# Mixing one batch directly ahead of another batch's scores, with other product steps and another beginning, in a fused decoder layer

## The chip, the cores and the metric

The kernel runs on one core of one Trainium2 chip. The metric is the device time of one execution in microseconds (us); the time before is the median of three runs.

## The reference

A decoder layer (self-attention, cross-attention to a context, MLP) is followed by a gated cross-attention to the same context. There are 16 batches of 128 tokens, 512 features, 16 heads of 32, all in float32.

```python
ln_out = layernorm(hidden_states, ln1_s, ln1_b)
q, k, v = jnp.split(ln_out @ w_qkv + b_qkv, 3, axis=-1)
ctx = merge_heads(attention(split_heads(q), split_heads(k), split_heads(v), ltor_mask))
x = hidden_states + ctx @ w_ao + b_ao
q = layernorm(x, ln2_s, ln2_b) @ w_q + b_q
k, v = jnp.split(encoder_states @ w_kv + b_kv, 2, axis=-1)
x = x + merge_heads(attention(split_heads(q), split_heads(k), split_heads(v), cross_mask)) @ w_co + b_co
x = x + gelu(layernorm(x, ln3_s, ln3_b) @ w1 + b1) @ w2 + b2
...
a = _layer_norm(audio_kv, ln_gamma, ln_beta)          # the same context
out = softmax_attention(hidden_states @ Wq.T, a @ Wk.T, a @ Wv.T, mask)
return hidden_states + jnp.tanh(gate) * (out @ Wo.T)
```

## The kernel before

**Stages and names.** The 16 batches form four groups of four (512 tokens). Self-attention is called A, the decoder's cross-attention B, the MLP C, the gated cross-attention D. A *section* is one group in one attention. `attend` is called twice: the decoder run has eight sections (A groups 0 to 3, then B groups 0 to 3, 32 batches), and after the MLP the gates' run has the four sections of D (16 batches).

**Order.** Every engine gets its instructions in the order in which the program writes them (`InOrder`), so the order below is the order in each engine's queue. Nothing is scheduled by a planner.

**Steps.** `attend` counts steps k; a section is 16 steps, a batch four, and one step is one *unit* of four heads. Batch b's units 4b to 4b+3 go through a pipeline: scores for all 16 heads at step 4b (`scores`, tile sc, 32 matmuls with 32 rows), scaling and masking of one unit per step, least value and exponential one step later, division by the sum two steps later, and three steps later `turn_unit`, which transposes 32x32 squares on VectorE and sends the unit to DRAM (tile away). `receive_pair` brings two units back with four DMAs on SyncE's queue, so that probabilities arrive transposed (tile pT, three buffers). It runs at step pair + 5, that is 4b+6 and 4b+8. `mix` multiplies them with the values (tile av, 32 matmuls of 32 columns) at step 4b+10, in the middle of a batch's four steps; its copy out of PSUM (`mixed_out`, ScalarE, tile mT) is put off to the next step by `afterwards` and `due`. The out-projection (mo) follows at the next step that starts a batch, 4b+12. In the gates' run the last batch isn't sent: TensorE turns it (`turn_by_array`) and it is mixed seven steps after its first unit's step.

**Products.** Beside the softmax of one section TensorE makes the queries, keys and values of the next. Each 512x512x512 product is split into seven quarter products (one level of Strassen's scheme), numbered 1 to 7, of eight 128x256 matmuls each. `block_product` puts 1, 6 and 7 into PSUM bank mm0 with a copy by ScalarE, 5 and 3 into mm1, 2 and 4 into the two pt buffers, with additions on VectorE one step later. Tables (`BLOCKS`, `SECOND_BLOCKS`, `CROSS_BLOCKS`, `GATED_BLOCKS`, `DEFERRED_BLOCKS`, and `FIRST_BLOCKS` for the first section) say at which step which quarter product is issued; `blocks_plan` turns them into lists. Sums of weights and of activations that the scheme needs run on GpSimd (tiles sums) or VectorE. In D the out-projections of groups 0 to 2 are deferred: their mixed tiles go to DRAM and come back, `added_product` makes them beside group 3 (mm_o_D), and `add_later` makes their sums on GpSimd.

**Beginning.** `SelfAttention.begin` loads x, normalizes group 0 batch by batch (statistics on VectorE, the power on GpSimd), transposes each batch on TensorE (tp_A), and copies the four transposed tiles out whole (`transposed_out`, ScalarE and VectorE in turn, tile T_A). `start` then issues seven query and seven key quarter products (mm_q_A, mm_k_A) before the first scores.

Of the kernel before, what the change touches and what calls it, by code (L numbers as in the profile page):

```python
# [10 lines left out]
F32 = mybir.dt.float32  # L11
# [5 lines left out]
P = 128  # L17
# [7 lines left out]
KC = H // P  # L25
GB = 4
# [27 lines left out]
def decoder_then_gated_cross_attention(ctx: ExitStack, tc: tile.TileContext, a: dict, out: bass.AP):  # L54
# [24 lines left out]
    def afterwards(engine, do):  # L79
        late[engine].append(do)  # L80
# [31 lines left out]

    for b in range(GB):
        load_batch(0, b)
# [37 lines left out]
    def col(name, c):  # L152
        cols, row = columns[name]
        return cols[:, row + c : row + c + 1]
# [3 lines left out]
    w["sq"] = load_weight(a["L0_xattn_w_qkv"], 0, 0, "w_sq")  # L158
# [49 lines left out]
    def normalize(src, dst, name, then):  # L208

        mv = work.tile([P, 2], F32, tag="mv", name=f"mv_{name}", bufs=4)  # L210
        st = work.tile([P, 6], F32, tag="st", name=f"st_{name}", bufs=4)
        nc.vector.bn_stats(st, src)
        nc.vector.bn_aggr(mv, st)
        rstd = work.tile([P, 1], F32, tag="rstd", name=f"rstd_{name}", bufs=4)
        nc.vector.tensor_scalar(rstd, mv[:, 1:2], EPS, None, ALU.add)
        nc.gpsimd.tensor_tensor(rstd, rstd, mhalf[:, 0:1], ALU.pow)

        def rest():
            to, of = (by_chunk(dst), squares(src)) if len(dst.shape) == 4 else (dst, src)
            nc.vector.tensor_scalar(to, of, mv[:, 0:1], rstd, ALU.subtract, ALU.mult)  # L220
            then()

        def rest_by_act():

            off = work.tile([P, 1], F32, tag="off", name=f"off_{name}", bufs=4)
            nc.vector.tensor_scalar(off, mv[:, 0:1], rstd, -1.0, ALU.mult, ALU.mult)
            nc.scalar.activation(by_chunk(dst), squares(src), AF.Identity, bias=off, scale=rstd)
            afterwards("dve", then)

        afterwards("dve", rest if at_start[0] else rest_by_act)  # L230
# [16 lines left out]
    def normalize_and_send(src, dst, away, name, b, then=None):  # L247
        def turn_and_send():
            nc.vector.transpose(dst, dst)
            send(away, dst, b)  # L250
            if then is not None:
                then()

        normalize(src, dst, f"{name}_{b}", turn_and_send)
# [50 lines left out]

    def transposed_out(t, tp, scale, bias):
        for k in range(KC):
            if k % 2 == 0:
                nc.scalar.activation(t[:, k, :], tp[k], AF.Identity, bias=col(bias, k), scale=col(scale, k))
            else:  # L310
                nc.vector.tensor_scalar(t[:, k, :], tp[k], col(scale, k), col(bias, k), ALU.mult, ALU.add)
# [149 lines left out]
    def by_quarters(t):  # L461
# [4 lines left out]
        {1: (1, 2), 2: (6,), 3: (7, 5), 5: (4,), 6: (3,)},  # L466
        {5: (1,), 6: (2,), 7: (6,), 9: (7, 5), 10: (4,), 13: (3,)},
        {10: (1,), 11: (6, 2), 13: (7,), 14: (5,), 15: (4, 3)},
    )

    FIRST_BLOCKS = (
        {0: (1, 2), 1: (6, 5), 2: (7, 4), 3: (3,)},
        {3: (1,), 4: (6, 2), 5: (7, 5), 6: (4, 3)},
    )
    SECOND_BLOCKS = (
        {4: (1, 2), 5: (6, 5), 6: (7, 4), 8: (3,)},
        {7: (1, 2), 8: (6,), 9: (7, 5), 10: (4,), 11: (3,)},
        {12: (1,), 13: (6, 2), 14: (7, 5), 15: (4, 3)},
# [3 lines left out]
        {6: (1,), 7: (6, 2), 9: (7, 5), 10: (4,), 11: (3,)},  # L482
        {11: (1,), 13: (6, 2), 14: (7, 5), 15: (4, 3)},
    )
    GATED_BLOCKS = (
        {0: (1,), 1: (2, 6), 2: (5, 7), 3: (4,), 5: (3,)},
        {5: (1,), 6: (2, 6), 7: (7,), 8: (5,), 9: (4,), 10: (3,)},
        {11: (1, 2), 12: (6,), 13: (5, 7), 14: (4,), 15: (3,)},
# [4 lines left out]
        {12: (1,), 13: (2, 6), 14: (5, 7), 15: (4,), 17: (3,)},  # L493
    )

    def blocks_plan(products, blocks, as_listed=False):
        out = {}
        for jobs, steps_ in zip(products, blocks):
            for step, ns in steps_.items():
                out.setdefault(step, []).extend((not as_listed and n not in (1, 6, 7), jobs[n]) for n in ns)  # L500
        return [([job for _, job in sorted(jobs, key=lambda j: j[0])], [step] * len(jobs)) for step, jobs in out.items()]
# [107 lines left out]
    def mix(bt):  # L609
        sec, b = bt.sec, bt.b  # L610
        av = ps("mm", f"av_{bt.name}")
        for c in range(KC):
            for j in range(GB):
                h = c * GB + j
                nc.tensor.matmul(
                    av[j * HD : (j + 1) * HD, c * S : (c + 1) * S], sec.v[:, b, h * HD : (h + 1) * HD],
                    bt.pT[j][:, :, c, :], start=True, stop=True,
                )
        mT = work.tile([P, KC, S], F32, tag="s", name=f"mT_{bt.name}", bufs=7) if bt.by_array else sec.mixed_tile(b)

        def mixed_out():
            if sec.v_bias is None:
                nc.scalar.copy(mT, av.rearrange("p (c q) -> p c q", q=S))
            else:
                for c in range(KC):
                    nc.scalar.activation(
                        mT[:, c], av[:, c * S : (c + 1) * S], AF.Identity, bias=col(sec.v_bias[0], sec.v_bias[1] + c)
                    )

        afterwards("act", mixed_out)  # L630
        bt.mT = mT
# [30 lines left out]
    def attend(sections, ready, others, after=None):  # L662
# [9 lines left out]

        def by_transfer(n):

            return min(n, (len(sections) * GB - 1) * GB) if ready else n

        def step(k, bt=None, jobs=(), ahead=None):

            m = k % GB
            pair = k - 5  # L680
            if pair % 2 and 0 <= pair < by_transfer(len(units)):
                receive_pair(*units[pair])
            if m == 0 and bt is not None:
                scores(bt)
            due()
            for job in jobs:
                job()
            last_mix = ready and k == by_transfer(k) + 7
            if last_mix:
                mix(batches[-1])  # L690
                projected.append(batches[-1])
            if projected and (m == 0 or ready and bt is None):
                before = projected.popleft()
                if before.by_array:
                    out_project_last(before)
                elif before.sec.deferred:
                    afterwards("act", lambda: before.sec.put_away(before))
                else:
                    out_project(before)
            done = k // GB - 2  # L700
            first_turned = ready and k == by_transfer(k) + 6
            if first_turned:
                turn_by_array(*units[k - 3])
            if m == 2 and 0 <= done < len(batches) - ready:
                mix(batches[done])
                projected.append(batches[done])
# [22 lines left out]
        for i, sec in enumerate(sections):  # L729
            last = i + 1 == len(sections)  # L730
            jobs = others() if last else sections[i + 1].jobs()
# [25 lines left out]
    class SelfAttention(Section):  # L757
# [19 lines left out]
        def begin(self, following):  # L777
# [3 lines left out]
            tp = []  # L781
            for b in range(GB + 1):
                if b == 1:
                    turn_vectors(0)
                    tp += [ps("sc", f"tp_A0_{k}") for k in range(KC)]
                left = late["dve"].popleft() if b else None
                if b < GB:
                    normalize(x[0][:, b, :], ln[:, b, :], f"A0_{b}", lambda b=b: transpose_batch(tp, ln, b))
                if left is not None:
                    left()  # L790
# [11 lines left out]
            for o in SelfAttention.weight_sums[0]:  # L802
                nc.gpsimd.tensor_tensor(*o)
            following.prepare(0)
            at_start[0] = False
            transposed_out(self.lnT, tp, "ln1_s", "ln1_b")

        def start(self, following):

            self.begin(following)  # L810
            _, todo = self.tiles()
            for o in todo:
                nc.vector.tensor_tensor(*o)
            key_sums, value_sums = self.weight_sums[1:]
            prepare = [lambda p=p: following.prepare(p) for p in (2, 4, 6, 9)], [0, 1, 2, 5]
            jobs = plan(
                *blocks_plan(self.products(), FIRST_BLOCKS), prepare,
# [28 lines left out]
        def jobs(self):  # L846
# [3 lines left out]
            if g > 1:  # L850
# [4 lines left out]
                *blocks_plan(first.products()[2:], FIRST_BLOCKS), (sums, [2, 3, 4, 5]),  # L855
# [33 lines left out]
    class CrossAttention(Section):  # L889
# [34 lines left out]
        def jobs(self):  # L924
# [9 lines left out]
            if g == 0:  # L934
# [6 lines left out]
                ([lambda c=c: self.query_chunk(c) for c in range(KC)], [1, 2, 3, 5]),  # L941
                *blocks_plan(products, CROSS_BLOCKS), ([lambda: mask_terms(self.ms, self.ma)], [7]),
# [18 lines left out]
        def weights_begin(self):  # L961
# [13 lines left out]
            def v_sum(n):  # L975
# [6 lines left out]
                ([lambda n=n: v_sum(n) for n in range(4)], [9, 10, 11, 12]),  # L982
# [406 lines left out]
    class GatedAttention(Section):  # L1389
# [110 lines left out]
        def jobs(self):  # L1500
# [16 lines left out]
            elif g == 3:  # L1517
                more = self.deferred_start()
            return plan(
                *blocks_plan(products, GATED_BLOCKS, True), ([by_pool(o) for o in a_sums], [0, 1, 2, 3]), ([mask], [9]), *more  # L1520
# [32 lines left out]
        def deferred_jobs(self):  # L1553
# [6 lines left out]
            def product(g, n):  # L1560
# [11 lines left out]
                ([lambda g=g: add_later(g) for g in (1, 2) for _ in range(4)], [0, 1, 2, 3, 8, 9, 9, 10]),  # L1572
                *blocks_plan(later, DEFERRED_BLOCKS, True),
# [134 lines left out]
```

## Time and profile before

| | |
|---|---|
| median of three runs | 1166.83 us (1165.11 to 1167.07) |
| profiled execution, its own time | 1168.78 us |
| its span, first to last instruction | 1167.0 us |
| mean granted TensorE clock | 0.994 |
| PE (TensorE matmul) busy | 1134.5 us, 97% |
| DVE (VectorE) busy | 739.2 us, 63% |
| ACT (ScalarE) busy | 605.6 us, 52% |
| POOL (GpSimd) busy | 701.5 us, 60% |
| DMA | 259.80 MB, mean 223 GB/s |
| first scores start | 39.73 us |

SP is SyncE, whose queue issues nearly all DMAs; SPq and PEq are the queues' own rows. A row of the timeline gives the start, the duration, the engine, the operation with output <- inputs, the shapes, the number of instructions in the row, and in brackets the idle time before it with what ended it. All operations pass through one helper, so every row has line L50, and tiles tell them apart. Suffixes A, B, C and D name the stage. The profiled execution is one run: its durations are held against its own time, 1168.78.

### The profile page before, as it was taken

What the parts mean: (1) busy time and instruction counts of PE and PEld (TensorE: products, weight loads), DVE (VectorE), ACT (ScalarE), POOL (GpSimd) and SP (SyncE); (2) the same over time, 40 slices, a digit from 0 to 9 for tenths busy, and PEclk for the clock granted to TensorE, in tenths of its full rate; (3) what the DMA queues carried; (4) which work ended last, traced back from release to release, by engine and by line L of the source; (5) the groups of instructions that cost most, each with busy time, mean ns of one, the idle gap of its engine ahead of it and who ended that gap; (6) DMA issues with size and microseconds to landing.
All of it is one profiled execution on the core that took longest, in us unless ns stands there. A gap on an engine that the chain in (4) does not pass through costs nothing. (4 is left out here: it accounts for less than half of the span.)

```text
span 1167.0 us, 22047 instructions
## 1 busy us (share of the span) xinstructions
PE 1134.5 (97%) x7210; PEld 868.3 (74%) x7210; DVE 739.2 (63%) x1894; ACT 605.6 (52%) x2132; POOL 701.5 (60%) x636
## 2 busy tenths in 40 slices
PE   7999999999999999998999999999999999999988
PEld 5877777657575757545788888888888777878866
DVE  7678878797878877876663633543432247767753
ACT  2467667666666766674221333232222247867653
POOL 7698878688868776684333424433341367545973
PEclk9999999999999999999999999999999999999989
DMA  6598979999889879898796696696457728988964
GB/s 227 148 221 220 240 188 222 248 235 267 199 229 208 239 202 255 243 290 252 264 287 235 188 273 197 193 301 224 154 184 249 211 48 229 249 215 251 264 191 163
DMA packets 325266, 259.80 MB, mean 223 GB/s; under 512 B 83544, under 2 KB 280608, under 8 KB 320288
## 3 DMA queue, kind: packets, MB, share of 16 engines
q1 hardware_dynamic: 325112, 258.38, 78.0%
q8 instruction: 58, 0.95, 0.3%
q14 instruction: 56, 0.46, 0.1%
q10 hardware_dynamic: 40, 0.01, 0.0%
HBM read 163.94 MB, written 94.37 MB: 221 GB/s over the span
## 5 line engine op out<-in xcount | busy, mean ns | idle before, releaser
L50 ACT ACTIVATE s_A<-s_A,mn_A 128x128 f32<-128x128 f32 x256 | 99.5, 393 | 51.5 <-issue 37.3
L50 DVE TENSOR_TENSOR h<-h,h 128x512 f32<-128x512 f32 x80 | 54.9, 686 | 112.6 <-PE h L50 112.6
L50 ACT ACTIVATE s_B<-s_B,mn_B 128x128 f32<-128x128 f32 x256 | 99.5, 393 | 46.6 <-issue 32.5
L50 ACT ACTIVATE h<-h 128x512 f32<-128x512 f32 x64 | 40.3, 630 | 160.6 <-DVE h L50 160.6
L50 POOL TENSOR_TENSOR s_D<-s_D,sum_D 128x512 f32<-128x512 f32 x64 | 66.5, 1040 | 67.8 <-DVE sum_D L50 66.3
L50 ACT ACTIVATE s_D<-s_D,mn_D 128x128 f32<-128x128 f32 x256 | 99.2, 392 | 0.4 <-issue 0.4
L50 POOL TENSOR_TENSOR s_B<-s_B,sum_B 128x512 f32<-128x512 f32 x64 | 66.8, 1045 | 48.7 <-DVE sum_B L50 44.3
L50 POOL TENSOR_TENSOR s_A<-s_A,sum_A 128x512 f32<-128x512 f32 x64 | 66.6, 1041 | 36.0 <-DVE sum_A L50 35.3
L50 POOL TENSOR_TENSOR s_A<-s_A,ma 128x512 f32<-128x512 f32 x64 | 81.9, 1280 | 5.4 <-DVE s_A L50 3.7
L50 POOL TENSOR_TENSOR s_B<-s_B,mask 128x512 f32<-128x512 f32 x64 | 81.3, 1270 | 2.1 <-DMA away_B<-s_B 0.4
L50 POOL TENSOR_TENSOR rstd_aD<-rstd_aD,mhalf 128x1 f32<-128x1 f32 x12 | 6.6, 548 | 114.6 <-DVE rstd_aD L50 101.1
L50 POOL TENSOR_TENSOR sh<-h 128x512 f32<-128x512 f32 x32 | 40.7, 1272 | 50.9 <-ACT h L50 43.0
L50 PE MATMUL mo_B<-w_co,mT_B 128*128 128x512 f32 x128 | 60.5, 616 | 2.1 <-ACT mT_B L50 2.1
L50 PE MATMUL h<-T_C,t 128*128 128x256 f32 x256 | 60.7, 380 | 1.4 <-DVE h L50 1.4
L50 PE MATMUL h<-T_C,w 128*128 128x256 f32 x256 | 61.0, 381 | 0.8 <-DVE h L50 0.8
L50 PE MATMUL h<-sx,t 128*128 128x256 f32 x256 | 60.6, 380 | 0.0
L50 PE MATMUL o<-w,h 128*128 128x256 f32 x256 | 60.5, 379 | 0.0
L50 PE MATMUL o<-t,h 128*128 128x256 f32 x256 | 60.5, 379 | 0.0
L50 PE MATMUL o<-t,sh 128*128 128x256 f32 x256 | 60.5, 379 | 0.0
L50 PE MATMUL mo_A<-w_ao,mT_A 128*128 128x512 f32 x128 | 59.1, 604 | 0.0
L50 DVE CUSTOM_DVE_ANT_0 s_D<-sc_D,gmask 128x128 f32<-128x128 f32 x256 | 57.2, 283 | 0.9 <-DMA turned_x<-x_D 0.9
L50 PE MATMUL mm_q_B<-T_B,w_cq 128*128 128x512 f32 x128 | 57.3, 595 | 0.0
(324 smaller groups left out, 2986.1 us busy)
## 6 DMA issues: line engine op xcount, KB each, us to landing
t<-kept SPq DMA_DIRECT2D x24, 1024.0 KB, 6.9
away_A<-s_A SPq DMA_DIRECT2D x64, 256.0 KB, 3.0
pT_A<-away_A SPq DMA_DIRECT2D x128, 128.0 KB, 3.0
away_B<-s_B SPq DMA_DIRECT2D x64, 256.0 KB, 5.2
pT_B<-away_B SPq DMA_DIRECT2D x128, 128.0 KB, 3.6
away_D<-s_D SPq DMA_DIRECT2D x60, 256.0 KB, 3.7
pT_D<-away_D SPq DMA_DIRECT2D x120, 128.0 KB, 2.8
w<-in_L_xattn_w_dram SPq DMA_DIRECT2D x24, 512.0 KB, 5.6
```

The source lines that it names most:

```text
L50: return lambda *args, **kw: self.tc.keep_in_program_order(call(*args, **kw))
```

## The change

- **Mix.** In each run, batch b is mixed at step 4b+12, directly ahead of the scores of batch b+3 (mix, scores, receives, put-off work, then `mixed_out` at once, then products). Pairs are received at 4b+8 and 4b+10. The out-projection follows two steps after the mix. At each run's end the third-last batch comes one step sooner, the last two come two steps sooner; the gates' last batch stays where it was.
- **Products.** The tables name other steps, and products run in the order listed. The third deferred out-projection starts at step 9 instead of 12, its sums on GpSimd go to steps 9 to 11 (8 to 10 before). The query chunks of B go to steps 0, 1, 3, 5 (1, 2, 3, 5), one group of weight sums to 8 to 11 (9 to 12).
- **Beginning.** The first query weights are loaded in two halves around the fourth x batch. Eighteen identity matmuls (36 instructions) are put around the first transposes. The third batch's statistics go to ScalarE. Transposes are copied out in halves of 256 tokens, and the first two query products start after the first half. The key's products are interleaved with the query's, and the first value product comes ahead of the first scores.

In all TensorE gets 18 matmuls more (3640 for 3622, two instructions each but for the transposes), VectorE 3 instructions fewer, ScalarE 8 more, GpSimd and SyncE one more each.

```diff
     BLOCKS = (
-        {1: (1, 2), 2: (6,), 3: (7, 5), 5: (4,), 6: (3,)},
-        {5: (1,), 6: (2,), 7: (6,), 9: (7, 5), 10: (4,), 13: (3,)},
-        {10: (1,), 11: (6, 2), 13: (7,), 14: (5,), 15: (4, 3)},
+        {0: (1,), 1: (2, 6), 2: (5,), 3: (7, 4), 5: (3,)},
+        {4: (1,), 5: (2,), 7: (6, 5), 8: (7,), 9: (4,), 11: (3,)},
+        {9: (1,), 11: (2,), 12: (6,), 13: (5, 7), 15: (4, 3)},
     )
...
     CROSS_BLOCKS = (
-        {6: (1,), 7: (6, 2), 9: (7, 5), 10: (4,), 11: (3,)},
-        {11: (1,), 13: (6, 2), 14: (7, 5), 15: (4, 3)},
+        {4: (1,), 7: (2, 6), 8: (5,), 9: (7, 4), 11: (3,)},
+        {10: (1,), 11: (2,), 12: (6,), 13: (5, 7), 15: (4, 3)},
     )
...
     DEFERRED_BLOCKS = (
...
-        {12: (1,), 13: (2, 6), 14: (5, 7), 15: (4,), 17: (3,)},
+        {9: (1,), 11: (2, 6), 13: (5, 7), 15: (4,), 17: (3,)},
     )
...
+        for b in range(len(sections) * GB):
+            k, at = (b + 3) * GB, (b + 2) * GB
+            sooner = min(2, max(0, b + 4 - len(sections) * GB))
+            k, at = k - sooner, at - sooner
+            if ready and b * GB == last:
+                k = last + 7
+            else:
+                for half in range(2):
+                    received_at.setdefault(at + 2 * half, []).append(b * GB + 2 * half + 1)
+            mixed_at[k] = b
...
-            pair = k - 5
-            if pair % 2 and 0 <= pair < by_transfer(len(units)):
-                receive_pair(*units[pair])
+            pairs, done = received_at.get(k, []), mixed_at.get(k)
+            beside_scores = done is not None and m == 0
+            if beside_scores:
+                mixed_out = mix(batches[done])
             if m == 0 and bt is not None:
                 scores(bt)
+            for pair in pairs:
+                receive_pair(*units[pair])
             due()
+            if beside_scores:
+                mixed_out()
+                projected.append((k, batches[done]))
...
-            if m == 2 and 0 <= done < len(batches) - ready:
-                mix(batches[done])
-                projected.append(batches[done])
+            if done is not None and not (beside_scores or last_mix):
+                afterwards("act", mix(batches[done]))
+                projected.append((k, batches[done]))
...
+            def keep_going(n):
+                for _ in range(n):
+                    nc.tensor.matmul(warm[:, 0:P], ident, ident, start=True, stop=True)
...
+            keep_going(8)
+            rest = [normalize(*args(b), True) for b in range(2)]
+            factor, rest_beside = normalize_beside(*args(2))
+            rest[0]()
+            turn_vectors(0)
+            keep_going(4)
+            turned(0)
+            keep_going(2)
+            rest[1]()
+            turned(1)
+            keep_going(4)
+            half_out(0, range(KC))
...
+                ([query[1], token_sums, query[2]], [0] * 3), ([query[5], query[6]], [1] * 2), ([key_early, query[7], query[4]], [2] * 3),
+                ([key[1], query[3]], [3] * 2), ([key[6], key[5]], [4] * 2), ([key[7], key[4]], [5] * 2),
+                ([key[3], self.values[1]], [6] * 2),
...
-                ([lambda g=g: add_later(g) for g in (1, 2) for _ in range(4)], [0, 1, 2, 3, 8, 9, 9, 10]),
-                *blocks_plan(later, DEFERRED_BLOCKS, True),
+                ([lambda g=g: add_later(g) for g in (1, 2) for _ in range(4)], [0, 1, 2, 3, 9, 10, 10, 11]),
+                *blocks_plan(later, DEFERRED_BLOCKS),
```

## Prediction

> **What bounds the kernel now.** I read the page first: which engine fills the span, and where its clock sags.
>
> ```profile
> PE 1134.5 (97%) x7210; PEld 868.3 (74%) x7210; DVE 739.2 (63%) x1894; ACT 605.6 (52%) x2132; POOL 701.5 (60%) x636
> ...
> PEclk9999999999999999999999999999999999999989
> ```
>
> TensorE fills 97% of the 1167.0 us span, so a gain must come out of PE: fewer or shorter gaps, or cheaper order. The chain of waits is no help (the page follows it over 3% of the span), so next I listed every PE start-to-start interval. Undisturbed, a 128x256 matmul takes 216 ns, a 128x512 one 429, a transpose 109; what exceeds these, apart from the regular cost of switching block kinds below, sums to some 36 us: beginning 7.4 (5.5 before 15.3, 1.9 at 22.3); eight places from 61 to 440, 6.8; the decoder run's end (524 to 539), 6.2; MLP, 3.0; the gates' first group (968 to 980), 2.8; 1029, 3.4; 1125 to 1135, 5.7. The timeline of PE in the beginning:
>
> ```profile
> 11.65 5.56 PE L50 MATMUL mm_q_A<-T_A,w_sq 128*128 128x256 f32 x16 [0.23 <-ACT T_A L50]
> 17.04 1.89 PE L50 MATMUL mm_q_A<-sums_A,sums 128*128 128x256 f32 x8
> 18.77 1.89 PE L50 MATMUL mm_q_A<-sums_A,w_sq 128*128 128x256 f32 x8
> 22.27 1.99 PE L50 MATMUL mm_q_A<-T_A,sums 128*128 128x256 f32 x8 [1.61 <-ACT q_A L50]
> ...
> 39.73 1.17 PE L50 MATMUL sc_A<-k_A,q_A 32*128 32x128 f32 x32
> ```
>
> Eight matmuls (one quarter product) take 18.77 - 17.04 = 1.73 us. The first two products take 17.04 - 11.65 = 5.39 instead of 3.45, since matmuls start 427 ns apart until 15.3. At 22.27 PE waits for an ACT copy. Then PE in the middle of a run, and the one place where a mix (av) stands directly before scores (sc):
>
> ```profile
> 127.96 1.08 PE L50 MATMUL av_A<-pT_A,v_A 128*32 128x128 f32 x32
> 128.97 1.99 PE L50 MATMUL mm_k_A<-sums_A,sums 128*128 128x256 f32 x8
> 130.89 1.17 PE L50 MATMUL sc_A<-k_A,q_A 32*128 32x128 f32 x32
> ```
>
> ```profile
> 1123.40 1.08 PE L50 MATMUL av_D<-pT_D,v_D 128*32 128x128 f32 x32
> 1124.41 0.49 PE L50 MATMUL sc_D<-k_D,q_D 32*128 32x128 f32 x4
> ```
>
> Between mix and scores the product takes 130.89 - 128.97 = 1.92, not 1.73: leaving one 32-wide block and entering the next costs 0.19 to 0.20 us. Standing together, the mix goes over into scores after its usual 1.01, with no such cost. Now PE's larger waits:
>
> ```profile
> PE sc_D L50 <- DVE mn_D L50: 4.3, 3, 3.2
> PE av_D L50 <- DMA pT_D<-away_D: 3.3, 2, 2.7
> ...
> PE mo_B L50 <- ACT mT_B L50: 2.1, 1, 2.1
> ```
>
> (Total us, times, longest.) Last, who could come next, by windows (PE, PEld, DVE, ACT, POOL, clock, DMA), and SP's queue:
>
> ```profile
> 102.00:163.00 61.00, 60.21 (x460) 44.31 (x457) 49.46 (x105) 42.11 (x167) 48.64 (x45) 1.00 0.84 218
> ...
> 1118.00:1131.00 13.00, 9.63 (x117) 7.71 (x116) 7.31 (x42) 8.76 (x42) 11.84 (x11) 0.88 0.76 221
> ```
>
> ```profile
> SPq L50 <- DMA away_D<-s_D: 34.7, 28, 2.9
> SPq L50 <- DMA away_B<-s_B: 33.0, 20, 7.1
> ```
>
> In a plain section DVE and POOL have 11 to 12 us of room in 61; in 1118 to 1131 POOL (11.84 of 13) is the bound, and PE waits for the softmax behind it.
>
> **Part by part**, against the profiled run of 1168.78 us (1.95 above the median 1166.83).
>
> *Mix ahead of scores.* The work is the same, only joined: program order has 42 mix-score neighbours instead of 1, so 41 x 0.195 = **-8.0**. The lower bound is zero saved, if the neighbours are torn apart by a wait. [...]
>
> *What the later mix delays.* Its probabilities are fetched by SP at steps 4b+8 and 4b+10 instead of 4b+6 and 4b+8. SP no longer blocks as long on a landing that it issued two steps before (these are the 34.7 and 33.0 above), but the mix now stands in PE's order ahead of the scores and of every product of that step: a late fetch stops all of it, and the softmax waits too. From first issue to landing a fetch takes 2.8 to 6.4, mostly 4 to 5 us. SP's free time at step 4b+10 lies 7 to 9.5 us ahead of those scores in the decoder (4.0 for the first batch), 3.2 to 5.3 in the first gated group, 5.9 to 8.8 later. So waits of about 1 us are expected for the very first batch and for two gated ones: **+1** and **+2**, bounds 0 and 6. The mixed copy on ACT goes out in the mix's own step instead of the next, and the out-projection follows two steps after the mix; the copy took 1 to 2 us, so PE's next use is covered by a whole step (some 3.8 us).
>
> *Product tables.* The instructions are the same. Of the 6.8 us from 61 to 440, nearly all are products that wait for an ACT or DVE copy from the bank they refill (1.14 at 81.7, 1.05 at 156 and 217, 1.2 at 252 and 438). Another step between them lets a 0.4 to 0.7 us copy pass. Equal moves elsewhere can create such waits: bounds 0 and -6.8; I take **-5**.
>
> *Beginning.* 14 products stand before the first scores, 15 afterwards (the first value product too): so 39.73 compares as 39.73 + 1.73 = 41.5. Query products start after two transposed batches instead of four. The second batch's transposes ended at 8.98; leaving out the statistics between them saves half a microsecond, one 128x256 ACT copy takes 0.42, so the start is 9.0 to 10.7 (the latter if w_sq, landed at 10.2, holds it); I take 9.5. Fifteen products are 25.9. Lost now after 11.65 are 1.94 (427 ns spacing) and 1.9 (wait at 22.3); I take half, 1.9: 9.5 + 25.9 + 1.9 = 37.3, **-4.2**. Best: 9.0 and nothing lost, -6.6; worst: 10.7 and all lost, -1.0. Batch 2's statistics move to ACT, some four instructions of at most 0.7 us (an estimate from its 0.63 us for a 128x512 activation), inside ACT's 7.57 us of idle time before its first copy at 10.82: nothing on PE's path. The 36 added identity matmuls (213 ns cold) lie in PE's idle time before 9. If they don't lift the clock, up to 17 more matmuls run at 427; that is in the worst bound. [...]
>
> *Decoder end.* Softmax of the last batches runs through POOL without a gap from 522 to 537; mixes two steps nearer there only keep the old place. Bounds 0 and -6.2: **-1.5**.
>
> *Gates.* The 3.4 at 1029 is a mix that waits for its fetch, then 427 ns spacing; two steps later the fetch is in: **-2.5**. First group, 2.8: **-1.5**. At 1118 to 1131 POOL's deferred sums (1.27 each) go one step later and the third deferred group's first product moves from step 12 to 9, which spreads what collides: 5.7 at stake, **-3.5**, bounds 0 and -5.7. MLP: unchanged.
>
> Sum: -8.0 + 3 - 5 - 4.2 - 1.5 - 2.5 - 1.5 - 3.5 = **-23.2**, 1168.78 - 23.2 = 1145.6. By the median it would be 1143.6; I say **1146**.
>
> **Rivals.**
> *Stalls only move* (chance 0.2): neighbours join and the beginning gains little, but each wait goes to the next product. -8.0 - 1.0 = -9: 1160. For it: DVE and POOL are 80% busy in plain sections. Against: several waits sit behind one copy in one bank.
> *Slower: the mix waits for its fetch* (0.08): in PE's queue at step 4b+12, with scores and products behind it, in every batch. If the 7 to 9.5 us of lead were eaten because SP receives later, each of 42 mixes would lose 1 us: 42 - 23 = +19, 1188. It decides from 23.2 / 42 = 0.55 us per mix on. For it: the gated leads of 3.2 against fetches of 4 to 5. Against: decoder leads are twice the fetch.
> *POOL takes over* (0.04): sums put off pile up at the runs' ends; the 11.84 of 13 stays and grows by 4 sums of 1.27: the gain shrinks to about -16, 1153.
>
> **How the numbers follow.** My forecast has 0.68, rivals 0.2, 0.08, 0.04. Low end: transitions 8, beginning 6.6, tables 6.8, gates and decoder end 12 (two thirds of their 18.1), new waits 0: -33, 1136. High end: the moved stalls, 1160. A measurement tells about 0.2% (2.3 us) from nothing: faster by more than that 0.87, within 0.04 (from the moved stalls), slower 0.09 (the second rival, and 0.01 for stalls that multiply).
>
> **What would show it.** Right: 42 places where av is followed by sc after 1.01 us; first scores near 37 with one value product done; no PE wait of 2 us for pT_D or mT_B; PE's busy share up, idle PE below 15 us. Wrong: av rows split as "x4" and "x28" with a DMA releaser in many batches (the slower rival); waits of products for ACT or DVE as many as before (moved stalls); POOL without gaps around the last scores; 427 ns spacing past 15.

## The result and the profile after

The changed kernel takes 1172.26 us (median of ten runs, 1168.88 to 1174.04) against 1166.53 us for the kernel before: 1.0047 times the time, 95% interval 1.0033 to 1.0062. It is 5.7 us slower where some 20 us less was forecast. The profiled execution has a span of 1172.1 us.

The page of the changed kernel: PE's busy row, and the granted clock by slice.

```profile
PE 1132.6 (97%) x7246; PEld 875.0 (75%) x7246; DVE 737.7 (63%) x1891; ACT 612.3 (52%) x2142; POOL 698.4 (60%) x637
...
PEclk9999999999999999998999999999999999999899
```

PE is busy 1.9 us less although it got 36 matmul instructions more, and the span is 5.1 longer. So PE idles more (39.5 us of the span, 32.5 before), and the clock sags in two slices (the 8s, around 540 and 1100 us) where it was full before; the one slice that sagged before (around 1123) is full now. Next the list of PE's waits in the changed kernel (total us, times, longest):

```profile
PE mo_B L51 <- ACT h L51: 7.8, 2, 6.9
PE av_D L51 <- DMA pT_D<-away_D: 7.0, 4, 4.3
PE av_B L51 <- DMA pT_B<-away_B: 3.8, 1, 3.8
PE mm_v_D L51 <- DVE v_D L51: 3.3, 3, 1.4
PE mm_k_D L51 <- DVE q_D L51: 1.8, 1, 1.8
```

Before, the longest after the first 5 us was 3.2 (sc_D for VectorE, gone now). The waits of av for a fetch were 3.3 (D) and 2.4 (B) in total, now 7.0 and 3.8; that of mo_B for ACT was 2.1, now 7.8, and for another tile, h. PE's loss can be added up from start-to-start intervals: what exceeds 216 ns (128x256), 429 ns (128x512), 109 ns (a transpose), 1.01 us for a mix, 1.10 us for scores and the cost of switching kinds. From its first product on PE loses 52.1 us that way, where it lost 36.8: 15.3 more. The joined blocks give back 8.0, the first product starts 3.2 us sooner (8.50 for 11.65), and eight transposes (0.9) now stand behind it: 15.3 - 8.0 - 3.2 + 0.9 = 5.0, which is the longer span.

**Where it goes, by milestones.** Starts of a batch's scores in the PE timelines, before and after: first batch 39.73 and 37.88; fifth (second section) 101.7 and 99.9; 30th 489.4 and 482.3; 32nd (the decoder's last) 515.0 and 514.2; first gated batch 947.9 and 950.6; last instruction 1167.0 and 1172.1. A lead of 7.1 us at 482 has become a lag of 2.7 at the first gated batch (9.8 us lost at the decoder's end), and another 2.4 are lost in the gates.

Three places of the changed kernel's PE timeline carry it. The first is the mix of the decoder's 28th batch:

```profile
493.86 0.41 PE L51 MATMUL av_B<-pT_B,v_B 128*32 128x128 f32 x4
498.07 1.92 PE L51 MATMUL av_B<-pT_B,v_B 128*32 128x128 f32 x28 [3.79 <-DMA pT_B<-away_B]
499.92 2.09 PE L51 MATMUL sc_B<-k_B,q_B 32*128 32x128 f32 x32
```

Four matmuls of the mix find the first pair, the others wait 3.79 us for the second; scores stand behind them. Then mix and scores run at half rate (1.92 and 2.09 instead of about 1 and 1.17): the granted clock is 0.50 from 496.6 to 503.5. From the start of the mix to that of the scores 6.06 us pass instead of 1.01, and with the slow scores and product behind them 6.7 us are lost by a wait of 3.8. SP's queue in the changed kernel tells when that pair was asked for:

```profile
490.22 2.94 SPq L51 DMA_DIRECT2D pT_B<-away_B  x4
```

That is 3.6 us ahead of the mix, and it took until 498, 7.8 us from the first issue (the four issues alone took 2.94). The second place is the out-projection of the 30th batch, beside the MLP's first product (tile h):

```profile
522.36 1.08 PE L51 MATMUL av_B<-pT_B,v_B 128*32 128x128 f32 x32
523.37 1.99 PE L51 MATMUL h<-T_C,w 128*128 128x256 f32 x8
532.22 6.35 PE L51 MATMUL mo_B<-w_co,mT_B 128*128 128x512 f32 x8 [6.86 <-ACT h L51]
```

ACT's copies at that place:

```profile
526.56 1.11 ACT L51 ACTIVATE mT_B<-av_B,vcols 128x128 f32<-128x128 f32 x4
531.35 0.81 ACT L51 ACTIVATE h<-h,vcols 128x256 f32<-128x256 f32 x2
```

The out-projection's input mT_B is ready at 527.7, yet it waits until 532.2 for ACT's copy of h. In the last decoder section mixes and out-projections take PSUM banks in turn (mm0, pt, mm1, pt). In the kernel before, this out-projection took a pt bank; with mix and out-projection in another order the turn gives it bank mm0, which the MLP's product has just filled. ACT reaches that copy only behind the softmax of the last batches. With half-rate matmuls behind it 9.8 us are lost. The third place is in the gates, again a fetch:

```profile
1094.68 0.41 PE L51 MATMUL av_D<-pT_D,v_D 128*32 128x128 f32 x4
1099.36 1.92 PE L51 MATMUL av_D<-pT_D,v_D 128*32 128x128 f32 x28 [4.26 <-DMA pT_D<-away_D]
1101.21 2.09 PE L51 MATMUL sc_D<-k_D,q_D 32*128 32x128 f32 x32
```

Where nothing is late the mix goes over into scores as forecast, with no cost between them:

```profile
513.18 1.08 PE L51 MATMUL av_B<-pT_B,v_B 128*32 128x128 f32 x32
514.19 1.17 PE L51 MATMUL sc_B<-k_B,q_B 32*128 32x128 f32 x32
```

That is 1.01 us from start to start. The trace has 42 such neighbours, as the prediction said, and 34 of them take 1.01.

### The profile page after: what moved, and what is told of

Its sections match the earlier page's. It is cut to its first block, busy times and chain, and to the rows that moved or that the text cites. A ratio compares the mean times of both kernels' runs of the same rounds, so it can differ in the third digit from the quotient of the medians.

```text
span 1172.1 us, 22142 instructions
## 1 busy us (share of the span) xinstructions
PE 1132.6 (97%) x7246; PEld 875.0 (75%) x7246; DVE 737.7 (63%) x1891; ACT 612.3 (52%) x2142; POOL 698.4 (60%) x637
## 4 chain that ended last, share of the span: by engine, by line
PE 44%; DMA 5%; POOL 3%; issue 2%; DVE 2%; ACT 2%; SPq 1%; POOLq 0%; DVEq 0%; ACTq 0%
PE h L51 16%; PE o L51 16%; PE mm_q_D L51 2%; DMA pT_D<-away_D 2%; PE mm_k_D L51 2%; PE mo_B L51 1%; PE mm_o_D L51 1%; SPq L51 1%; PE mm_v_D L51 1%; PE mo_D L51 1%; PE av_D L51 1%; POOL s_D L51 1%; DVE s_D L51 1%; DMA mixed<-kept_mT_D 1%; ACT s_D L51 1%
## 5 line engine op out<-in xcount | busy, mean ns | idle before, releaser
L51 PE MATMUL h<-T_C,w 128*128 128x256 f32 x256 | 61.1, 381 | 0.8 <-DVE h L51 0.8
```

The source lines that it names most:

```text
L51: return lambda *args, **kw: self.tc.keep_in_program_order(call(*args, **kw))
```

## The experiments

Twelve kernels ran, each against the kernel before on the same chip. Theory A grew out of the three places: two new waits, one for a PSUM bank and one for late fetches, eat the gain. Its rivals: the ends of the runs are set by softmax anyway, or the tables cost.

**The bank alone** (in the changed kernel).

```diff
     def out_project(bt):
+        if bt.name == "B3_1":
+            flip[0] = (flip[0] + 3) % 4
```

> The changed kernel, but the order of PSUM banks is moved by three places just ahead of the out-projection of the decoder's 30th batch (second of the last group), so that it no longer shares bank mm0 with the MLP's first product (h). Theory A (the bank is what PE waits for at 525 to 532): the 6.9 us wait for ACT's h goes, and most of the 2.9 us of half-rate matmuls behind it; the decoder's end is bound next by the last fetches, so 5 to 9 us less than the changed kernel, about 1163 to 1167. Rival B (softmax through POOL and ACT sets the end of the decoder run, whatever the bank): the wait moves to the next mix, under 1.5 us gained.

Measured: 1165.34 us, ratio 0.9985 (0.9973 to 0.9997). Against the changed kernel's 1.0047 that is 0.6%, 7 us, as theory A expected. PE's timeline of this run, same place:

```profile
523.25 1.99 PE L51 MATMUL h<-T_C,w 128*128 128x256 f32 x8
527.65 3.70 PE L51 MATMUL mo_B<-w_co,mT_B 128*128 128x512 f32 x8 [2.41 <-ACT mT_B L51]
```

The out-projection now starts when its own input is there, and at full rate (3.70, not 6.35). The edit shifts the turn for the four blocks behind it too, two mixes and two out-projections; what shows that the bank was the cause is that the wait for h is gone. One line of bank order brings the change back to the kernel before, or just under it. The wait at 498 is still there (6.6 lost).

**The receives alone** (in the changed kernel).

```diff
-            k, at = k - sooner, at - sooner
+            k, at = k - sooner, at - 2
```

> The changed kernel, but pairs of turned probabilities are received at 4b+6 and 4b+8, as in the kernel before; the mix stays at 4b+12. Theory A (mixes wait because the receive stands too late in SP's queue): the waits of av for pT at 267, 498, 989, 1013 and 1099 (13.7 us with the half-rate matmuls behind two of them) go: 9 to 13 us less than the changed kernel. Rival B (SP blocks at the earlier receive, or the DMA queues are full there, so that later transfers come late instead): under 4 us gained, with waits of other instructions in the same places.

Measured: 1164.81 us, 0.9982 (0.9971 to 0.9993), 7.5 us less than the changed kernel: between the two figures. The five waits of av at 267, 498, 989, 1013 and 1099 are gone, and the decoder's last scores start at 506.7 instead of 514.2. But PE's waits in this run show where part of it goes:

```profile
PE mo_B L51 <- ACT h L51: 10.1, 2, 9.2
PE mm_v_D L51 <- DVE v_D L51: 3.8, 3, 1.4
PE mm_q_D L51 <- ACT q_D L51: 2.2, 1, 2.2
```

PE comes to the bank wait earlier and waits longer there (9.2 instead of 6.9; 12.3 lost with the clock). In the gates ACT waits 3.64 us for the DMA kept_mT_D ahead of a copy that PE needs.

**Mix put back, tables and beginning as changed.**

```diff
-            sooner = min(2, max(0, b + 4 - len(sections) * GB))
+            sooner = 2
```

> The changed kernel with mix, receives and out-projection two steps earlier in every batch, so 42 mixes stand apart from scores again; tables and beginning as changed. Theory A: 8 us of joining are lost, 13.7 us of waits for pT and the bank wait (9.8) go: about 1157 to 1162. Rival B (the tables of products are what costs): still about 1172 or more, 1178 if joining is worth its 8 us.

Measured: 1186.11 us, 1.0175 (1.0153 to 1.0198). A missed by 24 us; B's "1172 or more" holds, but its figure of 1178 was 8 us too low. PE's waits in this run:

```profile
PE mm_k_B L51 <- ACT q_B L51: 8.9, 3, 3.2
PE mm_k_A L51 <- ACT k_A L51: 4.7, 2, 2.4
```

**Mix alone, in the kernel before** (the new `attend` and `mix`, nothing else).

> The kernel before, with only the new place of mix, receives and out-projection; tables and beginning as before. Theory A: joining saves 8, waits for pT and the bank at the decoder's end cost 15 to 20: 1171 to 1180. Rival B (tables cost, mixing gains): 1158 to 1162.

Measured: 1195.93 us, 1.0248 (1.0225 to 1.0272), 29 us slower, and 16 more than theory A had at most. av_D waits 15.9 us for fetches in five places, mo_B 7.9 for the same bank as above, and the waits of products for copies in the first sections rise (3.6 lost from 80 to 85 where 1.1 was lost before).

**Tables alone, in the kernel before.**

> The kernel before with only the new product tables and the shifted deferred sums; mix and beginning as before. Theory A (the tables are made for the mix at 4b+12, where an additional wait stands at the step that starts a batch; with the mix apart they cost as they did in the run with the mix put back): 1178 to 1192. Rival B (tables alone take the waits of products for copies away): 1160 to 1164.

Measured: 1185.59 us, 1.0155 (1.0133 to 1.0177), 18.3 us slower, as theory A expected; it loses in the same places as the run with the mix put back. PE's timeline:

```profile
377.58 1.17 PE L50 MATMUL sc_B<-k_B,q_B 32*128 32x128 f32 x32
381.92 2.44 PE L50 MATMUL mm_k_B<-T_e,w_ck 128*128 128x256 f32 x8 [3.16 <-ACT q_B L50]
```

The product's bank was filled by a query chunk that ended at 377.6, and ACT copied it out at 381.20, behind a mix's copy (1.11) and the exponentials of one unit, which waited for GpSimd and VectorE. In the changed kernel the same copy goes out at 359.16, 0.4 us after its chunk, and PE has mix and scores to do before the product. That this order of ACT's copies, with less PE work in between, is the reason in the other places too was not tested. So mix and tables belong together: alone they cost 29 and 18, together 6 (7 with the old beginning, run below).

**Bank and receives together.**

> Both edits together: the PSUM bank of the 30th batch's out-projection moved, and pairs received at 4b+6 and 4b+8. Measured alone they gave 6.9 and 7.5 us less than the changed kernel. Theory A (two separate waits; in the run with early receives the bank wait grew from 9.8 to 12.3 us of lost PE time, so it hides part of what early receives give): the sum or more, 14 to 19 us less, 1153 to 1158. Rival B (the decoder's end is bound by softmax, each edit only uncovers that): 9 us less or under, 1163.

Measured: 1157.64 us (1157.24 to 1158.73), 0.9917 (0.9898 to 0.9935): 14.6 below the changed kernel, about the sum of both parts (6.9 + 7.5), as theory A expected, and faster than both kernels. PE's waits in this run:

```profile
PE mm_v_D L51 <- DVE v_D L51: 5.9, 3, 3.1
PE mo_B L51 <- ACT mT_B L51: 4.3, 2, 3.8
PE h L51 <- DVE h L51: 2.5, 3, 1.0
PE mm_q_D L51 <- ACT q_D L51: 2.1, 1, 2.1
PE av_B L51 <- DMA pT_B<-away_B: 2.1, 2, 1.4
```

mo_B no longer waits for the copy of h but for its own input, ACT's copy mT_B, and that copy stands on ACT behind the exponentials of one unit. So the decoder's end still loses 10.4 us (510 to 537), 6.5 of them at mo_B. In all PE loses 36.8 us from its first product on, as much as in the kernel before (36.8). The profiled span is 10.4 us shorter, by the 8.0 of the joined blocks and the earlier first product (3.2 less 0.9): the stalls have moved without getting fewer.

**Receives in the gates only one step earlier.**

> As the run before, but the gates' run receives only one step earlier than in the changed kernel (4b+7, 4b+9). In the run with receives two steps earlier the gates lost 4.2 us at 1003 (ACT's copy mT_D waits for the DMA kept_mT_D, issued on SP behind the receives) and 2.1 at 1110 (a product's addition waits for the DMA x<-kept_x). Theory A (SP blocked on landings puts these DMAs off): one step later they go out in time, and leads of 5 us still cover most fetches: 2 to 6 us less than the run before, 1150 to 1154. Rival B (waits for pT come back at 989, 1013, 1099): within 2 us of the run before or longer.

Measured: 1165.48 us, 0.9978 (0.9964 to 0.9991). Theory A fell: 7.8 us more than the run before, which is as long as the bank edit alone (1165.34). The waits of products for v_D sum to 6.9 us (5.9 in the run before; the one at 986.5 is 2.50 long, and the quarter product behind it takes 3.64 instead of 1.99), and one fetch is late again by 2.0, near 1090. In its profile PE loses 4 us more than in the run before, half of the 8: the profiled execution took 1162.21, 3.3 below the median, so its trace cannot show the rest. Why one step earlier in the gates gives nothing isn't settled.

**Receives early in the decoder and for one gated batch** (the edit is shown against the run with both edits).

```diff
-            k, at = k - sooner, at - 2
+            k, at = k - sooner, at - (max(sooner, 2 * (b == 9)) if ready else 2)
```

> The bank edit, receives at 4b+6 and 4b+8 in the decoder's run, and in the gates for the tenth batch alone; the gates' other batches as in the changed kernel. Theory A (one late fetch, at 1099, is most of what early receives gain in the gates; the small waits at 989 and 1013 are worth as much as ACT's wait that early receives bring): within 2 us of the run with both edits, 1156 to 1160. Rival B (the small waits of the gates add up): 1161 to 1165.

Measured: 1159.25 us, 0.9940 (0.9922 to 0.9959). As A expected: 1.6 us above the run with both edits by the medians, 2.7 by the ratios. Fetches cost av_D 3.3 us in five places (the longest 1.5), and the waits for v_D fall to 3.0, from 5.9. So in the gates an early receive for the one late batch does nearly as well as for all. No run has early receives in the decoder alone, so how much that one batch is worth by itself isn't shown.

**The beginning alone, in the kernel before.**

> The kernel before with only the new beginning (load order, identity matmuls, third batch's statistics on ACT, halves, interleaved products, first value product ahead of the first scores); mix and the other tables as before. Theory A (the beginning is worth what the milestones show: first scores at 37.9 instead of 39.7 with one more quarter product done, half of it lost again by 100 us): 2 to 4 us less than before, 1163 to 1165. Rival B (what is gained before the first scores is lost in the first section's softmax): within 1 us of before.

Measured: 1166.49 us, 1.0001 (0.9987 to 1.0014): nothing. PE's timeline shows first scores at 38.10 with a quarter product more done, 3.4 us ahead, and then

```profile
60.94 1.97 PE L51 MATMUL mm_q_A<-T_A,sums 128*128 128x256 f32 x8 [1.43 <-ACT q_A L51]
68.10 1.17 PE L51 MATMUL sc_A<-k_A,q_A 32*128 32x128 f32 x32
```

a product waiting for ACT's copy, which stands behind exponentials and a normalization, and the third batch's scores at 68.1 against 68.8 before. Rival B holds.

**The old beginning in the changed kernel, and the changed kernel without identity matmuls.**

> The changed kernel with the beginning of the kernel before (load order, whole copies, no identity matmuls, 14 quarter products ahead of the first scores). Theory A (the beginning's 3.6 us are lost again in the first section, as in the run of the beginning alone, which was as long as before): 1171 to 1174. Rival B (with the mix ahead of scores the early start is kept): 1175 to 1177.

> The changed kernel without its 36 identity matmuls. Theory A (they lift the clock before the products: matmuls are 216 ns apart from 8.5 on): without them the first transposes and products run at 427 ns for some 4 us, first scores near 39.5 instead of 37.9, but the first section's softmax swallows most of it: 1172 to 1174. Rival B (the clock lifts early by the transposes alone): first scores still at 38, 1172.

Measured: 1172.82 us (1.0059, 1.0042 to 1.0075) and 1172.21 us (1.0047, 1.0028 to 1.0066), both as the changed kernel. Without identity matmuls the first query product takes 3.29 us instead of 1.89 (half rate from 8.20), but the second starts at 12.45 instead of 12.39: in the changed kernel PE is ready sooner, and then the fourth batch's transposes wait for VectorE until 11.90. So the first scores start at 37.9 in both, not at 39.5 as theory A of that run had it. Nor did the clock lift as early as its rival B had it, since the first product still ran at half rate.

**Quarter product 7 one step earlier in the gated values** (in the run with both edits).

```diff
-        {9: (1,), 10: (2,), 11: (6, 5), 13: (7,), 14: (4,), 15: (3,)},
+        {9: (1,), 10: (2,), 11: (6, 5), 12: (7,), 14: (4,), 15: (3,)},
```

> The run with both the bank and the receive edits (1157.6), and the gated values' quarter product 7 moved from step 13 to 12. Theory A (in the gates steps 14 and 15 have lost the mix that stood between products; PE comes to product 3 before VectorE has added the fourth quarter out of bank mm1, which needs product 7's copy: 1.7, 3.4 and 1.6 us of waits at 986, 1037 and 1084): these waits go, 4 to 6 us less, 1152 to 1154. Rival B (the softmax chain behind ACT's wait for kept_mT_D holds VectorE, whatever the order): 1156 or more.

Measured: 1158.01 us, 0.9934 (0.9916 to 0.9952): no gain on the run with both edits. The waits for v_D are gone, and others have come:

```profile
988.43 0.93 PE L51 MATMUL sc_D<-k_D,q_D 32*128 32x128 f32 x6
990.92 2.04 PE L51 MATMUL sc_D<-k_D,q_D 32*128 32x128 f32 x26 [1.55 <-DVE mn_D L51]
```

Scores now wait for VectorE to empty their banks, as they did before at 1125. PE had been held by a product, now by the softmax itself, as rival B had it; the wait for kept_mT_D that B names as the reason was not taken out in any run. (The profiled execution, 1161.78, is the longest of the six.)

## Why the prediction was wrong

Two terms failed: the later receive, priced at +3 with at most 6, and the out-projection that was "covered by a whole step". Taking both waits out made the kernel 14.6 us faster.

*Joined blocks, -8.0: right.* A section from the sixth batch on takes 59.3 us (116.0 to 175.3) where it took 61.1 (116.3 to 177.4) with one stall of 1.05; the difference without it is 0.75, four times 0.19.

*The later receive, +3 with bounds 0 and 6: the step that failed first.* In five places, at 267, 498, 989, 1013 and 1099, the mix took 2.33, 6.06, 2.32, 2.92 and 6.53 us up to the scores where 1.01 is usual. That is 15.1 us, or 18.1 with the half rate behind two of them (the 13.7 in the expectations counts less of the half rate). Two errors made it. The leads were read from the kernel before, from SP's free time at 4b+10 to the scores at 4b+12, with the mix still standing between; joined with the scores it is reached sooner. At the 28th batch the rows before give a lead of 5.9 (SP free at 496.25, scores at 502.17), already under the 7 that the prediction has as the least, and it became 3.6; at the tenth gated batch 6.2 became 2.5. And a fetch was taken at its usual 4 to 5 us, at most 6.4; in these two places it took 7.8 and 7.2 from the first issue. DMA engines were busy for 0.98 of the stretch from 480 to 545, but for 0.96 of it in the kernel before too, so load alone does not explain it. SP did lose its blocking on landings, as forecast, but it waits for VectorE's turned units instead (35.9 and 33.0 before):

```profile
SPq L51 <- DVE s_D L51: 71.3, 36, 9.8
SPq L51 <- DVE s_B L51: 45.2, 29, 4.2
```

(SP's waits in the changed kernel.) A receive stands behind the sends of the step before in SP's queue, so it cannot be ahead of the softmax. Just ahead of the receive at 490.22, though, SP issues almost without a pause from 481 on (no wait of half a microsecond), so there the length of its queue counts. The rival that the mix waits for its fetch named place and mechanism, but as one of "every batch"; it is five of 42, and the price was 3.6 us each, not 1, partly because of the clock.

*Out-projection "covered by a whole step", decoder end -1.5: the second step that failed.* Only the time of ACT's copy was counted. From 523 to 539 the kernel before lost 6.9 us; the changed one loses 9.8 there in a single wait. A reordering also reorders the hand-out of PSUM banks, and no step of the sum looked at which bank each block gets. The run with the bank moved showed 7 us for it.

*Tables, -5: half of it, and taken back by the beginning.* From 40 to 440 us the product waits sum to 6.6 us (7.1 before). But from 100 on they fall from 4.8 to 2.5. It is from 40 to 100 that they rise, from 2.2 to 4.2, and this goes with the new beginning: the run with the beginning alone has 4.7 there, the run with the old one 1.8. The runs with tables and mix alone show that the sum of separate terms was the wrong form: the tables lose 18.3 without the mix, and the mix 29 without them.

*Beginning, -4.2: right up to the first scores (3.6), nothing behind them.* What comes next had been left out: in the first section products wait for ACT's copies, which stand behind other work of ACT (1.43 at 60.9).

*Gates.* The stalls at 1029 and 1125 to 1135 went as forecast (9.1 us), and the first group's fell from 3.5 to 2.1. Others came: besides the fetch at 1099, 4.1 at v_D's products and 2.9 at the end. This was the rival "stalls only move", given 0.2. With the two new waits mended the kernel lands at 1157.6, 2.4 us under that rival's 1160; nothing that ran came near 1146.

*Readings and sums.* The prediction's list of stalls leaves out scores and mixes that run at half rate: counted in, the stall at 1029 is 4.5 us, not 3.4, and that at 1125 to 1135 is 7.2, not 5.7. Its 1146 is set off from the profiled run; from the median its own sum gives 1143.6. And the rival in which POOL takes over comes to -23.2 + 3.5 + 5.1 = -14.6, not -16. None of this decides the outcome.

## What to carry to other kernels

When instructions are reordered, list which buffer or bank each one gets by rotation before and after, and who empties the bank it inherits: one step of rotation was worth 7 us here. Look at terms together that share a queue or an engine's order: here two parts that each cost 18 and 29 us alone cost 6 together. A receive's lead has to be worked out with the new order and the fetch times of that stretch, not with what is usual in the run. Where PE is 97% busy and in order, price a stall by who is late next, and count a recovered wait as zero until the next engine's chain is seen to have room.

## What the hardware showed

The three longest PE waits of the changed kernel cost more than their length. Counted from start to start, with what ran at half rate behind it, the wait of 3.79 us at 498 cost 6.7, that of 4.26 at 1099 cost 6.9, and that of 6.86 at 532 cost 9.8: 2.6 to 2.9 us more each time. In all three the granted clock was 0.50 for 6.8 us; at 498 it fell at 496.6, when PE had been idle for 2.4 us. Slow matmuls came after shorter waits too: after 2.73 at 1029 in the kernel before, the clock was 0.50 for 3.4 us (28 matmuls of a mix in 1.92 instead of 1.07), and after 3.16 in the run with tables alone a quarter product took 2.44 instead of 1.99 and the out-projection behind it 4.89 instead of 3.60. A single wait of 1.81 at 972 in the changed kernel was followed by none: the quarter product behind it took 1.99, and the clock stayed at 1.00.

That the 36 matmul instructions on a constant lift the clock before data arrive was shown too (products run 216 ns apart from 8.50 on; without them the first took 3.29 us instead of 1.89), and that it brought nothing, since the transposes behind it waited for VectorE (0.80, until 11.90).
